# Transposes of a Perceiver-style kernel moved from TensorE to 32 by 32 blocks on VectorE, with copies and DMAs between the blocks

## The chip, the core and the metric

The kernel runs on one core of a Trainium2 chip. The metric is the device time of one execution in microseconds, taken as the median of several executions. A profile is one further execution recorded by the hardware profiler; its rows have times in us unless they are marked ns. The engines are PE (TensorE), DVE (VectorE), ACT (ScalarE), POOL (GpSimd) and SP (SyncE, which here only issues DMAs).

## The reference, cut to what matters

The input is x, 32 sequences of 64 tokens of width 256, and a context of 32 sequences of 256 tokens of width 256. Six residual blocks follow each other, all in float32:

```python
x = x + L0_xattn(ctx, layernorm(x))   # 16 heads of 64; keys and values from normalized context and x
x = x + L0_attn(layernorm(x))         # linear attention, 16 heads of 16
x = x + L0_ffn(layernorm(x))          # gated, hidden width 768
x = x + L1_xattn(layernorm(x), ctx, ctx, mask)   # 16 heads of 16, softmax over 256 context tokens
x = x + L1_attn(layernorm(x))         # sLSTM over the 64 tokens
x = x + L1_ffn(layernorm(x))          # 8 experts of width 1024, entmax gates
```

In both cross attentions, the softmax runs over the context tokens, so scores come out with the queries on the partitions and the context along the row. The product with the values sums over the context, so it needs the probabilities with the context on the partitions. That turn, and the turn of the context itself for the first attention's keys, are the transposes of this study.

## The kernel before

Tokens are held in 16 tiles of 128 (two sequences each), and all 16 stay in SBUF. The work falls into three stages.

**First cross attention** (`l0_context` to `l0_projected`, from line 774). It loops over the 16 tiles and in each over two batches. `l0_queries` handles a group of four batches at a time: it forms queries (banks `pq`) and folds the key weights into them (banks `pqk`, tiles `qk`). So scores are taken against the normalized context itself: `l0_keys` (line 855) turns the context of one batch with four PE transposes into a bank `tr_c` and copies it to the tile `cT`; a copy on POOL adds the 64 own tokens. `l0_scores` (line 869) forms eight banks `sc` of 128x320, takes a maximum on DVE and an exponential on ACT for each, scales on DVE, and turns the probabilities without PE: DVE transposes 32x32 blocks into `bT`, and 16 moves, one for each pair of block row and block column, carry the blocks into `pT`. Four of the moves are POOL copies, four go to ACT or DVE, and eight are DMAs. `l0_applied` (products `pu`) and `l0_projected` (`po`, `pw`) follow.

**Middle stage.** It loops over eight groups of two tiles: `linear_attention` (line 1092, names beginning with la), `feed_forward` (ff), `queries` (`xaq`), then for each tile `keys_values` (line 1245: loads the context already transposed, `ctxT`, into `xcT`, and forms `xak` and `xav`), and for each half of the heads `scores` (line 1274, banks `xsc`) and `weighted` (line 1313). `weighted` turns the probabilities with 16 PE transposes into four banks `xpTp`, copies each to SBUF, turns the reciprocal sums (`xrT`), and forms the products `xpo`. It then adds the value bias `vb` as it joins the two head halves. `projected` (`xpw`) and `slstm_router` (line 1365) follow.

**Experts.** The first twelve tiles' tokens go through gates and a first pass over eight experts, then the last four tiles' tokens and what was left over.

**What sets the order.** The kernel doesn't issue its instructions as it meets them. A planner (`Plan`, line 210) collects every operation with a rank, and `Plan.run` (line 299) lays them out one by one: of the operations whose inputs and places are there, it takes the one that can start first by its own table of durations (`PlanEngine.length`, line 474), and of equal ones that of lower rank. An operation whose rank is more than `ahead` (12.0, line 1863) above the lowest open rank has to wait. Operations given by `either` or `copy` may go to ACT or DVE. Each engine then runs its instructions in the order laid out, and SP issues its DMAs in that order too. Most instructions carry line 375, where the planner emits them, so the profile's groups are told apart by the names of their tiles and by their shapes. All SBUF tiles but a few are places in one large area, `arena`, given by `ar.put` (from line 646) with a tag, a size and one position for each buffer; a place is free again when all readers of its last tile are done.

## Time and profile before

| | |
|---|---|
| median of 3 runs | 1628.32 us (1628.05 to 1630.23) |
| the profiled execution | 1633.02 us |
| its span, first to last instruction | 1631.3 us |
| mean granted PE clock | 0.991 of full speed |
| PE, PEld (weight loads) | 1579.4 us, 1106.8 us busy |
| DVE, ACT, POOL | 1088.2, 693.8, 422.1 us busy |
| DMA | 95.02 MB, mean 58 GB/s |

A row of the slices shows the busy share of an engine in tenths for each of 40 equal parts of the span. A row of groups has the engine, the operation, output and input by name and shape, and a count; then its busy time in us and the mean duration of one in ns; then how long the engine stood idle in front of such an instruction, and what ended that. PE's instructions overlap each other, so the busy time of a group is less than its count times its mean. A product in float32 stands as two records for each instruction of the program; a transpose stands as one. A row of stretches has the length in us, the busy time and the number of instructions of each engine, the granted clock, the share of time that the DMA engines were busy, and GB/s.

### The profile page before, as it was taken

What the parts mean: (1) busy time and instruction counts of PE and PEld (TensorE: products, weight loads), DVE (VectorE), ACT (ScalarE), POOL (GpSimd) and SP (SyncE); (2) the same over time, 40 slices, a digit from 0 to 9 for tenths busy, and PEclk for the clock granted to TensorE, in tenths of its full rate; (3) what the DMA queues carried; (4) which work ended last, traced back from release to release, by engine and by line L of the source; (5) the groups of instructions that cost most, each with busy time, mean ns of one, the idle gap of its engine ahead of it and who ended that gap; (6) DMA issues with size and microseconds to landing.
All of it is one profiled execution on the core that took longest, in us unless ns stands there. A gap on an engine that the chain in (4) does not pass through costs nothing. (4 is left out here: it accounts for less than half of the span.)

```text
span 1631.3 us, 25951 instructions
## 1 busy us (share of the span) xinstructions
PE 1579.4 (97%) x9226; PEld 1106.8 (68%) x9226; DVE 1088.2 (67%) x3089; ACT 693.8 (43%) x1813; POOL 422.1 (26%) x524
## 2 busy tenths in 40 slices
PE   8999999999999999999989999999999999999996
PEld 6556656565665656666556777777777776878885
DVE  6657666676766757776755788888888788762230
ACT  4434344353533535334421454454544547432332
POOL 5123123230333223331311221221212112223342
PEclk9999999999999999999999999999999999999998
DMA  6112112121112211122121000010000220455391
GB/s 212 38 30 59 38 31 44 38 59 29 39 30 46 47 34 40 30 71 53 38 54 49 14 27 27 18 37 14 27 27 20 85 80 19 133 144 141 69 307 31
DMA packets 95601, 95.02 MB, mean 58 GB/s; under 512 B 9327, under 2 KB 85936, under 8 KB 95472
## 3 DMA queue, kind: packets, MB, share of 16 engines
q1 hardware_dynamic: 89952, 85.41, 19.2%
q0 software_dynamic: 5520, 7.94, 2.4%
q8 instruction: 74, 1.21, 0.3%
q14 instruction: 55, 0.45, 0.1%
HBM read 63.63 MB, written 7.47 MB: 44 GB/s over the span
## 5 line engine op out<-in xcount | busy, mean ns | idle before, releaser
L375 PE MATMUL pu<-arena 128*128 128x512 f32 (+1 forms) x768 | 301.0, 615 | 3.5 <-ACT arena L375 2.8
L375 PE MATMUL sc<-arena 128*128 128x320 f32 x1024 | 290.5, 436 | 0.0
L375 PEld LDWEIGHTS sc<-arena 128*128 128x128 f32 x1024 | 190.8, 190 | 95.3 <-issue 19.2
L375 ACT ACTIVATE arena<-sc,nmax 128x320 f32<-128x320 f32 x256 | 134.4, 527 | 250.3 <-DVE nmax L375 241.8
L375 PEld LDWEIGHTS pu<-arena 128*128 128x128 f32 (+1 forms) x768 | 113.9, 189 | 175.9 <-issue 159.1
L375 POOL COPY arena<-arena 32x640 f32<-32x640 f32 (+1 forms) x161 | 108.9, 676 | 404.1 <-DVE arena L375 300.4
L375 DVE TENSOR_REDUCE nmax<-sc 128x1 f32<-128x320 f32 x256 | 121.8, 484 | 105.5 <-PE sc L375 104.1
L375 POOL TENSOR_TENSOR arena<-arena 128x1024 f32<-128x1024 f32 (+3 forms) x72 | 118.5, 1646 | 166.6 <-DVE arena L375 109.7
L375 ACT ACTIVATE arena<-arena,xnm 128x256 f32<-128x256 f32 x256 | 127.1, 500 | 52.1 <-DVE xnm L375 51.9
L375 DVE COPY arena<-pu 128x512 f32<-128x512 f32 x62 | 42.7, 689 | 115.4 <-PE pu L375 115.2
L375 DVE CUSTOM_DVE_ANT_0 arena<-xsc,arena 128x256 f32<-128x256 f32 x256 | 101.2, 421 | 17.7 <-ACT arena L375 10.3
L375 DVE TENSOR_TENSOR arena<-arena,sm 128x1280 f32<-128x1280 f32 x64 | 108.1, 1690 | 2.2
L375 DVE STREAM_TRANSPOSE arena<-arena 128x512 f32<-128x512 f32 (+1 forms) x192 | 104.4, 594 | 3.6
L375 ACT COPY arena<-pu 128x512 f32<-128x512 f32 x66 | 38.4, 585 | 128.0 <-PE pu L375 128.0
L375 POOL DMA_INDIRECT out<-arena x25 | 39.6, 1585 | 102.8 <-DVE arena L375 71.2
L375 PE MATMUL pqk<-arena 64*128 64x256 f32 x512 | 63.1, 383 | 1.6 <-ACT arena L375 1.6
L375 PE MATMUL xpTp<-ident,arena 128*128 128x128 f32 x512 | 63.6, 274 | 0.9 <-ACT arena L375 0.9
L375 PE MATMUL xak<-arena 128*128 128x512 f32 x128 | 62.3, 610 | 0.0
L375 PEld LDWEIGHTS xpTp<-ident,arena 128*128 128x128 f32 x512 | 56.9, 141 | 7.2 <-DVE arena L375 2.2
L375 PE MATMUL xav<-arena 128*128 128x256 f32 x256 | 61.5, 384 | 0.0
L375 PEld LDWEIGHTS po<-arena 128*64 128x64 f32 x1024 | 55.5, 137 | 8.8 <-issue 8.3
L375 PE MATMUL mepha<-arena 128*128 128x256 f32 x256 | 60.1, 385 | 1.4 <-ACT arena L375 1.4
(395 smaller groups left out, 2800.9 us busy)
## 6 DMA issues: line engine op xcount, KB each, us to landing
arena<-in_m_w SPq DMA_DIRECT2D x26, 1024.0 KB
arena<-arena SPq DMA_DIRECT2D x256, 80.0 KB
arena<-in_ctx SPq DMA_DIRECT2D x32, 256.0 KB
arena<-in_ctxT SPq DMA_DIRECT2D x16, 512.0 KB
x<-in_x SPq DMA_DIRECT2D x16, 128.0 KB
arena<-in_l0x_wkv SPq DMA_DIRECT2D x2, 1024.0 KB
arena<-arena SPq DMA_DIRECT2D x16, 128.0 KB
out<-x SPq DMA_DIRECT2D x16, 128.0 KB
```

Of the source, the lines that this page charges most:

```text
L375: r = getattr(real, name)(*[get(a) for a in args], **{k: get(a) for k, a in kw.items()})
```

## The change

- **Context keys of the first attention.** For batches 1 to 31 `l0_keys` no longer uses PE. Two DVE transposes of 128x256 turn 32x32 blocks of the context into a new tile `bC`, and 16 moves of 32x128 carry them into `cT`: four by POOL, twelve by ACT or DVE. Batch 0 keeps the PE transposes. The columns of `cT`, and with them the blocks of the probabilities, stand in another order.
- **Probabilities of the second attention.** The 512 PE transposes and the 128 copies of `xpTp` go. For each half of a tile's heads, two DVE transposes of 128x1024 write `xbT`, and 16 moves of 32x512 fill `xpT`: four by POOL, four by ACT, eight by DMA. `xpr` has three places of 1024 instead of two of 2048, `xpT` one of 2048 instead of four of 512, `xbT` one, and `xcT` one instead of two.
- **Value bias.** It is folded into the output bias once, with two products (`pvb`), and the join of the two head halves becomes an addition on POOL.
- **sLSTM.** In seven of the eight groups, four small DVE operations move to POOL.
- **Planner.** A lean of 0.1 us against DVE where an operation may go to ACT or DVE; POOL copies have a shorter duration in its table; `ahead` is 10.0 instead of 12.0.
- **Places and order.** `wk` and `q` get other places (`q` is four quarter tiles), the linear attention's weights `a_wq` and `a_wkv` move to the places of `q` and are loaded late in the first stage, and the heads' groups are processed in plain order.

The diff, cut to its core:

```diff
-                    key = at, op.rank
+                    key = at + (self.lean if engine == "DVE" and len(op.ways) > 1 else 0.0), op.rank
...
-            return 0.7 if n < 64 else 0.3 + 2.0e-3 * n
+            return 0.7 if n < 64 else 0.15 + 0.97e-3 * n if name == "tensor_copy" else 0.3 + 2.0e-3 * n
...
-        ar.put(1, "q", 2048, 8192)
+        ar.put(0, "wk", 2048, 25856)
+        ar.put(1, "q", 512, 8192, 8704, 9216, 9728)
+        ar.put(1, "bC", 512, 42496, 43008)
...
-            ("xcT", 1024, 22016, 23040), ("xkT", 1024, 24064, 25088), ("xv", 1024, 30208, 31232),
-            ("xpr", 2048, 26112, 28160), ("xpT", 512, 35328, 35840, 36352, 36864), ("xne", 256, 37376, 37632, 37888),
+            ("xcT", 1024, 22016), ("xkT", 1024, 23040, 24064), ("xv", 1024, 30208, 31232),
+            ("xpr", 1024, 25088, 26112, 27136), ("xbT", 2048, 28160), ("xpT", 2048, 35328), ("xne", 256, 37376, 37632, 37888),
...
-            ("a_wq", 512, 42496), ("a_wkv", 1024, 43008), ("rows_a", 1024, 44032),
+            ("a_wq", 512, 8192), ("a_wkv", 1024, 8704), ("rows_a", 1024, 44032),
...
             if t == 2:
 
+                pl.rank = 29.5
...
+        def move(n, o, i, tight=False):
+
+            if n == 0:
+                pl.gpsimd.tensor_copy(o, i)
+            elif n == 1 and tight:
+                pl.scalar.copy(o, i)
+            elif n == 1:
+                pl.copy(o, i)
+            else:
+                pl.sync.dma_start(out=o, in_=i)
...
+            pl.rank = b - 2.6
+            cT = ar.tile([P, 5, KD, S], F32, tag="cT", name=f"cT{b}")
+            pl.gpsimd.tensor_copy(cT[:, 4], lt[:, :, b4 * S : (b4 + 1) * S])
...
+            bC = ar.tile([P, 4, KD, 2, B_], F32, tag="bC", name=f"bC{b}")
+            for i in range(2):
+                pl.vector.transpose(
+                    bC[:, :, :, i].rearrange("p k d c -> p d k c"),
+                    cx[:, 2 * b2 + i].rearrange("p (d k c) -> p d k c", d=KD, c=B_),
+                )
+            for n in range(4):
+                for a in range(4):
+                    k = (a + n) % 4
+                    move(
+                        min(n, 1),
+                        cT[B_ * k : B_ * k + B_, a].rearrange("p d c -> p (d c)"),
+                        bC[B_ * a : B_ * a + B_, k].rearrange("p d i c -> p (d i c)"),
+                    )
...
+        pl.vector.tensor_copy(vd, vb.unsqueeze(2).to_broadcast([P, 2, P]))
+        pl.lane = "vb"
+        pvb = bank([P, D], "pvb")
+        with pl.together(0.9):
+            for c in range(2):
+                mm(pvb, vd[:, c], x_wo[:, c, :], start=(c == 0), stop=(c == 1))
+        pl.vector.tensor_tensor(row("x_bo"), pvb, row("x_bo"), ALU.add)
...
+                pl.vector.transpose(
+                    bT[:, :, b2].rearrange("p k d j c -> p j d k c"),
+                    pr.rearrange("p j (d k c) -> p j d k c", d=2, c=B_),
+                )
+            pT = ar.tile([P, 4, 2, 2, 4, B_], F32, tag="xpT", name=f"xpT{nm}")
+            for n in range(4):
+                for a in range(4):
+                    k = (a + n) % 4
+                    move(
+                        n,
+                        pT[B_ * k : B_ * k + B_, a].rearrange("p b d j c -> p (b d j c)"),
+                        bT[B_ * a : B_ * a + B_, k].rearrange("p b d j c -> p (b d j c)"),
+                        tight=True,
                     )
...
-            for b2 in range(2):
-                for kc in range(2):
-                    pT = ar.tile([P, 4, P], F32, tag="xpT", name=f"xpT{nm}_{b2}_{kc}")
-                    pT_ps = bank([P, 4, P], f"xpTp{nm}_{b2}_{kc}")
-                    with pl.together(T4):
-                        for j in range(4):
-                            tr(pT_ps[:, j, :], pr[:, b2, j, kc * P : (kc + 1) * P], ident)
-                    pl.copy(pT, pT_ps)
-                    pTs[b2, kc] = pT
...
-            pl.vector.scalar_tensor_tensor(
-                oT[:, c], om[:, :, 0, :], vb[:, c : c + 1], om[:, :, 1, :], ALU.add, ALU.add
-            )
+            pl.gpsimd.tensor_tensor(oT[:, c], om[:, :, 0, :], om[:, :, 1, :], ALU.add)
...
+            side = pl.vector if g == NG - 1 else pl.gpsimd
+            side.tensor_scalar(il[:, :, :, 1:], il[:, :, :, 1:], 20.0, None, ALU.min)
...
-        pl.run(12.0)
+        pl.run(10.0)
```

## The prediction

> **What bounds the kernel now.** I read the page first: the busy shares, then the slices, because a mean over a kernel of three stages can hide a different limit in each.

> ```profile
> span 1631.3 us, 25951 instructions
> ...
> PE 1579.4 (97%) x9226; PEld 1106.8 (68%) x9226; DVE 1088.2 (67%) x3089; ACT 693.8 (43%) x1813; POOL 422.1 (26%) x524
> ...
> PE   8999999999999999999989999999999999999996
> ...
> DVE  6657666676766757776755788888888788762230
> ...
> PEclk9999999999999999999999999999999999999998
> ```

> TensorE (PE) is at nine tenths or more in 37 of 40 slices, at the full granted clock. VectorE (DVE) is next, and the only engine that comes near in the second half (slices 23 to 34). So I cut the span into stages and asked for each engine's busy time in each: first cross attention, change-over, the middle stage with the second cross attention, experts.

> ```profile
> core 0: us, PE busy (x) PEld busy (x) DVE busy (x) ACT busy (x) POOL busy (x), PEclk, DMA share, GB/s
> ...
> 80.00:840.00 760.00, 756.56 (x3632) 472.90 (x3631) 511.22 (x989) 315.83 (x767) 207.12 (x209) 1.00 0.19 43
> 840.00:880.00 40.00, 34.13 (x192) 22.53 (x189) 24.66 (x73) 8.36 (x16) 9.54 (x20) 0.91 0.25 66
> 880.00:1410.00 530.00, 520.42 (x4007) 389.40 (x4007) 427.99 (x1574) 269.56 (x783) 100.74 (x185) 1.00 0.11 36
> 1410.00:1631.30 221.30, 199.20 (x1106) 173.79 (x1104) 70.75 (x330) 63.13 (x159) 74.20 (x63) 0.96 0.50 140
> ```

> In the first attention PE idles 3.4 of 760 us, in the middle stage 9.6 of 530. Every microsecond taken off PE there is one off the time, as long as the others keep up. The page's chain of waits is of no use here: it ends at the last store on POOL and shows 0%. Third came the groups by shape, for durations.

> ```profile
> L375 POOL COPY arena<-arena 32x640 f32<-32x640 f32 x128 | 98.1, 766 | 304.3 <-DVE arena L375 300.4
> L375 DVE STREAM_TRANSPOSE arena<-arena 128x512 f32<-128x512 f32 x128 | 83.5, 690 | 3.6
> L375 PE MATMUL xpTp<-ident,arena 128*128 128x128 f32 x512 | 63.6, 274 | 0.9 <-ACT arena L375 0.9
> L375 ACT COPY arena<-arena 32x640 f32<-32x640 f32 x64 | 46.2, 722 | 18.6 <-DVE arena L375 17.2
> L375 DVE COPY arena<-xpTp 128x512 f32<-128x512 f32 x60 | 40.0, 685 | 4.5 <-PE xpTp L375 4.3
> L375 ACT COPY arena<-xpTp 128x512 f32<-128x512 f32 x68 | 38.6, 587 | 39.9 <-PE xpTp L375 39.8
> L375 DVE STREAM_TRANSPOSE arena<-arena 128x256 f32<-128x256 f32 x64 | 25.8, 402 | 0.0
> L375 PE MATMUL tr_c<-ident,arena 128*128 128x128 f32 x128 | 18.7, 276 | 0.0
> ```

> [...]PE's operations overlap, so its price is the busy time, 63.6/512 = 0.124 us a transpose, not the 274 ns that one lasts.

> **The PE work that goes.** All 512 xpTp transposes: 63.6 us. Of the 128 tr_c transposes 124 (batch 0 keeps its four): 18.7 x 124/128 = 18.1. The folded bias adds two 128x256 products, four PE records at 58.7/256 = 0.23 us (the pw group): 0.9. Net 80.8 us. If nothing came in their place the end would be 1628.3 - 80.8 = 1547.5. The profiled execution took 1633.0 around its span of 1631.3; the median is 1628.3, 0.3% below. I subtract from the median; the scale changes the sum by 0.3 us.

> **What comes instead, second attention.** Counts are from the built order of the changed program. DVE: 64 transposes of 128x1024, which no row shows; from 128x256 at 402 and 128x512 at 690 the slope is 1.125 ns an element, so 402 + 768 x 1.125 = 1.27 us each, 81. Gone from DVE: 60 copies, 40; 32 additions of 128x128 to GpSimd (POOL) at 0.340, 11; four s-LSTM steps in seven of eight groups at 0.386 + 3 x 0.334, 10. The lean of 0.1 us against DVE sends about 100 either-engine operations to ACT (31 relus at 0.386, 19 normalizations at 0.408, the rest 0.42 to 0.74): 46. DVE goes from 428 to 428 + 81 - 40 - 11 - 10 - 46 = 402. ACT: -39, +128 moves of 32x512, +about 47 for those operations. For the moves the row at 32x640 (722 ns) gives 578 in proportion and 722 at most; 0.61 x 128 = 78. ACT 270 to 356. POOL: 128 moves at about 0.65, 32 additions and the s-LSTM steps at about 0.5 to 0.7: +110, to 211. PE falls to 520.4 - 63.6 = 456.8. So DVE stands at 88% of PE's work instead of 82%, ACT at 78%, POOL at 46%: PE is still the longest, by less.

> [...]

> **The new wait.** Scores, transposes, moves and product of one half form a chain. Its prices come from a timeline of the first attention, where the same moves exist:

> ```profile
> 601.61 1.63 DVE L375 STREAM_TRANSPOSE arena<-arena 128x512 f32<-128x512 f32 x3
> ...
> 616.15 5.44 SPq L375 DMA_DIRECT2D arena<-arena  x8
> ...
> 616.18 3.19 POOL L375 COPY arena<-arena 32x640 f32<-32x640 f32 x4 [18.80 <-DVE arena L375]
> ...
> 625.39 3.17 PE L375 MATMUL pu<-arena 128*128 128x512 f32 x7
> ```

> Eight issues take 5.4 us; the packets in the trace end 1.2 us after the last. Eight exponentials at 0.50 + 0.19 keep ACT 5.5 us and start about 1 us into the 2.7 us of score products, so the last ends some 4 us after them; then 1.3 for the second transpose, 5.4 + 1.2 + 0.3 for the moves: about 12 us. In the built order PE has 13.7 to 29.5 us of other work between a half's scores and its product. Alone the chain is covered; with DVE at 88% its eight reductions and two transposes queue behind others, and the tightest halves (13.7 to 15.5) can stall.

> SP's queue also carries context loads, stores and expert weights: 256 new issues, 166 us of 457. A load that waits for PE holds the moves behind it.

> xcT, the transposed context, now has one place instead of two. The load of tile t+1 waits for the last value product of t, and on PE only 0.5 to 0.9 us of work stands between that and the first key product at five of the 15 changes; 2.3 at one, 3.4 or more at nine. A load moves 512 KB; in the trace its packets end 3.0 to 3.4 us after issue (154 GB/s in such a stretch), with the hop about 3.5. Stalls: 5 x 2.7 + 1.2 = 15 us. Bounds: 0, if PE is held elsewhere just then, and 30, if the load also queues behind a set of moves.

> For DVE's tightness I let the idle share of PE double from 9.6/530 to 3.6%: 457 x 0.036 - 9.6 = 7 us. Bounds 0 and 25.

> **What comes instead, first attention.** 62 transposes of 128x256 at 0.402: 25 us on DVE, less copies of tr_c and those leaned away (18 of 32x640 at 0.834, 9 of pu, 7 of tr_c: 26), plus 67 copies of 32x128 (at 0.17 in proportion to 32x640 to 0.3 with a fixed part, 11 to 20): about 525 in all. ACT gets 305 copies of 32x128, +18 of 32x640, +9 of pu, -24 of tr_c. No row has the small copy. [...] Keys start one batch earlier in rank; the context's affine step ends at 630.7 where its scores start at 646.0, and the 16 moves need about 5 us. I charge 2 us, bounds 0 and 10.

> **Ends.** The loads of a_wq and a_wkv (768 KB) leave the start for the last batches and stand in SP's order a batch (25 us) ahead of their products: nothing. The expert stage keeps its work; its third weight place now also waits for keys and probabilities, and the planner looks 10 ranks ahead instead of 12: 3 us, bounds -3 and 8. Sum: 80.8 - 15 - 7 - 2 - 3 = 54. 1628.3 - 54 = 1574.5, say **1575**.

> **Rivals.** *Nothing is given back*: 1547 to 1555; speaks for it the first attention's near perfect cover with DVE at 67%, against it the single xcT. Chance 0.18. *VectorE becomes the bound*: DVE's 402 us are 50 a group of two tiles, and each half's pair of transposes must wait for one xbT. POOL can lengthen DVE too: one 128x1280 product took 1.49 us alone and 2.94 beside a POOL product. If DVE operations grow by a fifth, 402 becomes 482 + 9.6, the middle stage shortens by 38 instead of 64, and with the other costs (15 + 2 + 3) the end is 1593; if the stage does not shorten at all, only 16 are left: 1612. I take 1603, between them; chance 0.17. *The chain becomes the bound, slower*: single xbT and xpT make halves serial. A group took 67.4 us for four halves, so it decides from 16.9 us a half. With 5.5 of scores, 2.5 transposes, 6.9 moves, 1.2 product and 2.5 of queueing, 18.6: 74.4 a group, +7 x 8 = 56, less 16: 1668. Against it stands that the scores of the next half need neither buffer. Chance 0.06. *No difference* 0.02.

> **How the numbers follow.** The main case, 1558 to 1592, has 0.57; with the first rival and most of the second the range 1550 to 1608 leaves about 2 in 10 out. Faster by over 0.2% (about what a measurement here tells from no change) are the first three, 0.92; within 0.02, slower 0.06.

> **What would show it.** Right: no xpTp group, four tr_c; PE about 1499 us busy, its idle in the middle stage about 30 us, with waits of the xak products on a DMA of in_ctxT; POOL's and ACT's copies up, idle. Wrong: PE busy under 90% there with the xpo products waiting on DVE or moves (the chain), or DVE at nine tenths with PE waiting for it (VectorE), or idle in front of sc (first attention).

## The result and the profile after

The changed kernel takes 1697.95 us (median of 4, 1689.05 to 1701.73), the kernel before 1628.18 beside it: a ratio of 1.042, 95% interval 1.0395 to 1.0443. The forecast was 1575 with a range to 1608. The profiled execution took 1694.88 us, its span 1693.2.

The page of the changed kernel, the lines that were read before (busy time and share, then tenths in 40 slices):

```profile
span 1693.2 us, 25872 instructions
...
PE 1556.5 (92%) x8594; PEld 1063.1 (63%) x8594; DVE 1089.9 (64%) x3047; ACT 866.5 (51%) x2265; POOL 553.4 (33%) x836
...
PE   7899999999999999999888998989989877889996
...
DVE  7566667666676666666565688868768677634131
...
PEclk9999999999999999999999999999989886899998
```

No engine has taken PE's place: DVE kept its busy time (1090 us, 1088 before), ACT is busy for half of the span and POOL for a third. PE has holes from slice 20 on, and its clock, at nine tenths or more in every slice but the last before, falls below that in slices 30 and 32 to 35, down to six tenths. Both show again in the windows of the stages (columns as before: busy us of each engine, then the granted clock):

```profile
80.00:840.00 760.00, 735.51 (x3459) 455.28 (x3458) 512.48 (x1065) 396.16 (x1046) 225.32 (x318) 0.99 0.19 44
840.00:880.00 40.00, 34.37 (x127) 19.37 (x126) 24.21 (x65) 12.08 (x28) 8.51 (x14) 0.96 0.21 47
880.00:1410.00 530.00, 473.17 (x3274) 335.88 (x3272) 388.83 (x1312) 311.21 (x819) 183.09 (x335) 0.94 0.22 61
1410.00:1693.00 283.00, 247.24 (x1457) 206.74 (x1457) 112.63 (x481) 104.89 (x269) 102.74 (x113) 0.90 0.46 131
```

In the middle stage PE idles 57 of 530 us instead of 10, and the granted clock is 0.94. DVE is busy for 73% of that stretch, 81% before, so the rival "VectorE becomes the bound" is out. The trace lists the stretches in which the clock was at half; with PE's records that splits a span into three sums: PE's busy time as it would be at full clock, the time lost at half clock (half of PE's busy time there: products of 128x256 for xav start 0.427 us apart in those stretches of the changed kernel, 0.216 at full clock, by the medians), and PE's idle time.

| us | PE work at full clock | lost at half clock | PE idle | span |
|---|---|---|---|---|
| before | 1571.4 | 7.9 | 51.9 | 1631.3 |
| after | 1502.7 | 53.8 | 136.7 | 1693.2 |
| difference | -68.7 | +45.9 | +84.8 | +61.9 |

So the PE work did go. More than it saved came back as idle time, and half as much again as a slower clock. The landmarks of the work say where (each cell: length, of it idle + lost at half clock):

| stretch | before | after |
|---|---|---|
| start to the pu products of batch 7 | 236.2: 11.9 + 1.5 | 243.9: 21.6 + 4.6 |
| to those of batch 31 | 617.8: 7.9 + 1.7 | 629.5: 22.3 + 7.0 |
| to the first xpw product of the middle stage | 87.0: 0.8 + 0.0 | 100.4: 7.2 + 1.4 |
| to the first slp product | 49.1: 0.8 + 0.0 | 53.8: 3.0 + 0.0 |
| four groups of four batches | 269.6: 4.0 + 0.0 | 271.6: 25.6 + 13.7 |
| three more, beside the experts' first half | 168.4: 5.0 + 0.0 | 212.0: 37.7 + 25.4 |
| to the end | 203.1: 21.6 + 4.8 | 182.0: 19.3 + 1.7 |

The first attention lost 19 us, the stretch between the attentions 13, the way from there to the first slp product 5, the four steady groups gained nothing from 33 us of PE work less, and the last two rows, which share their work out differently, lost 22 together. What PE waited for in the two stages (engine, tile, what ended the wait: us, times, longest), first of the first attention, then of the middle stage:

```profile
PE pqk L375 <- ACT arena L375: 14.1, 14, 1.4
PE laq L375 <- ACT arena L375: 4.6, 1, 4.6
```

```profile
PE xak L375 <- DMA arena<-in_ctxT: 7.1, 3, 3.0
PE xrT L375 <- POOL arena L375: 6.0, 2, 5.8
PE xsc L375 <- DVE x L375: 5.0, 1, 5.0
PE xak L375 <- DVE ve_lay L375: 5.0, 2, 2.5
PE xsc L375 <- ACT arena L375: 4.0, 5, 1.3
PE xav L375 <- DVE xnm L375: 3.9, 1, 3.9
...
PE xak L375 <- DVE arena L375: 2.9, 1, 2.9
```

These are many waits of many kinds. The three rows of xak give 15.0 us together. In front of the value products xpo, which end the chain of scores, moves and product, PE waits only 2.9 us in all. The name behind the arrow is not always the last cause: in a timeline of the changed kernel one gap has two names, VectorE's at the weight load and the DMA's at the product.

```profile
1098.72 1.67 PE L375 MATMUL xav<-arena 128*128 128x256 f32 x7
...
1100.42 0.33 SPq L375 DMA_DIRECT2D arena<-in_ctxT  x1
...
1103.81 0.30 PEld L375 LDWEIGHTS xak<-arena 128*128 128x128 f32 x2 [2.96 <-DVE ve_lay L375]
1103.85 1.68 PE L375 MATMUL xak<-arena 128*128 128x512 f32 x2 [2.59 <-DMA arena<-in_ctxT]
```

The load is issued as the last product on the one place of xcT ends (1100.4), and the product that needs it starts 3.4 us later. The 128x1024 transpose was forecast well: it lasts 1.24 us (1.27). The 32x128 copy, of which no row of before told, lasts 296 ns on ACT, 255 on DVE and 287 on POOL.

### The profile page after: what moved, and what is told of

Same layout as the page of the kernel before. It is cut to its first block, busy times and chain, and to the rows that moved or that the text cites. A ratio compares the mean times of both kernels' runs of the same rounds, so it can differ in the third digit from the quotient of the medians.

```text
span 1693.2 us, 25872 instructions
## 1 busy us (share of the span) xinstructions
PE 1556.5 (92%) x8594; PEld 1063.1 (63%) x8594; DVE 1089.9 (64%) x3047; ACT 866.5 (51%) x2265; POOL 553.4 (33%) x836
## 4 chain that ended last, share of the span: by engine, by line
PE 27%; DVE 12%; ACT 5%; DMA 3%; POOL 2%; issue 2%; SPq 0%; DVEq 0%; POOLq 0%; ACTq 0%
DVE arena L375 7%; ACT arena L375 5%; PE mepya L375 3%; PE mepha L375 3%; PE ffg L375 2%; PE xak L375 2%; PE xav L375 2%; POOL arena L375 2%; PE pu L375 2%; PE ffu L375 2%; PE lakv L375 1%; PE sc L375 1%; PE mepyb L375 1%; DVE x L375 1%; PE mephb L375 1%
## 5 line engine op out<-in xcount | busy, mean ns | idle before, releaser
L375 POOL COPY arena<-arena 32x640 f32<-32x640 f32 (+3 forms) x413 | 220.9, 537 | 563.1 <-PE sc L375 257.6
L375 PE MATMUL pu<-arena 128*128 128x512 f32 (+1 forms) x768 | 300.8, 615 | 4.5 <-DMA arena<-arena 3.2
L375 PE MATMUL sc<-arena 128*128 128x320 f32 x1024 | 291.3, 437 | 1.5 <-DVE arena L375 1.2
L375 ACT COPY arena<-arena 32x128 f32<-32x128 f32 (+2 forms) x515 | 228.2, 443 | 61.6 <-DVE arena L375 50.1
L375 PEld LDWEIGHTS sc<-arena 128*128 128x128 f32 x1024 | 191.5, 190 | 96.7 <-issue 17.6
L375 ACT ACTIVATE arena<-sc,nmax 128x320 f32<-128x320 f32 x256 | 133.7, 526 | 184.2 <-DVE nmax L375 183.2
L375 PEld LDWEIGHTS pu<-arena 128*128 128x128 f32 (+1 forms) x768 | 114.1, 189 | 176.2 <-issue 156.1
L375 DVE STREAM_TRANSPOSE arena<-arena 128x512 f32<-128x512 f32 (+2 forms) x318 | 208.3, 691 | 16.8 <-POOL arena L375 10.6
L375 POOL TENSOR_TENSOR arena<-arena 128x128 f32<-128x128 f32 (+3 forms) x125 | 135.7, 1089 | 187.1 <-DVE arena L375 144.4
L375 DVE TENSOR_REDUCE nmax<-sc 128x1 f32<-128x320 f32 x256 | 120.5, 482 | 98.6 <-PE sc L375 95.6
L375 ACT ACTIVATE arena<-arena,xnm 128x256 f32<-128x256 f32 x256 | 127.3, 500 | 49.1 <-DVE xnm L375 48.9
L375 DVE CUSTOM_DVE_ANT_0 arena<-xsc,arena 128x256 f32<-128x256 f32 x256 | 101.7, 417 | 26.5 <-ACT arena L375 22.1
L375 ACT COPY arena<-pu 128x512 f32<-128x512 f32 x75 | 42.7, 586 | 113.6 <-PE pu L375 113.6
L375 DVE TENSOR_TENSOR arena<-arena,sm 128x1280 f32<-128x1280 f32 x64 | 96.6, 1509 | 2.2
L375 PE MATMUL pqk<-arena 64*128 64x256 f32 x512 | 70.3, 409 | 14.1 <-ACT arena L375 14.1
L375 PE MATMUL xak<-arena 128*128 128x512 f32 x128 | 69.2, 674 | 14.9 <-DMA arena<-in_ctxT 7.1
L375 DVE COPY arena<-pu 128x512 f32<-128x512 f32 x53 | 36.0, 681 | 67.5 <-PE pu L375 67.5
L375 PE MATMUL xav<-arena 128*128 128x256 f32 x256 | 72.2, 433 | 5.9 <-DVE xnm L375 3.9
L375 PEld LDWEIGHTS pqk<-arena 64*128 64x128 f32 x512 | 53.2, 199 | 31.2 <-ACT arena L375 21.5
L375 PE MATMUL mepha<-arena 128*128 128x256 f32 x256 | 65.7, 411 | 5.2 <-DVE xnm L375 2.7
L375 POOL DMA_INDIRECT out<-arena x25 | 39.7, 1589 | 92.6 <-ACT arena L375 61.5
L375 ACT ACTIVATE arena<-arena 128x256 f32<-128x256 f32 (+3 forms) x59 | 23.2, 397 | 89.8 <-DVE arena L375 86.6
```

The lines of the kernel that those rows point to most:

```text
L375: r = getattr(real, name)(*[get(a) for a in args], **{k: get(a) for k, a in kw.items()})
```

## Experiments

The theory after the traces (A): gaps on PE, most of them in the middle stage, cost their own length and the clock behind them. Rivals: B, the keys' part with its small copies; C, the planner's three new constants (the lean against DVE, the length of a GpSimd copy, `ahead` 10); D, the chain of moves; later E, the moves as blocks in ScalarE's queue, and A', that beside the experts the transposes had covered VectorE's chains. Medians are in us; the ratio is to the kernel before, timed beside each. That kernel's own median moved between 1628.15 and 1633.59 from one session to the next, so where two runs come from different sessions, a difference of their medians can be off by some 5 us. The planner rearranges other work after most edits, so a single edit is rarely alone; where it was, the text says so.

### The two halves and the planner

**second_only**: keys of all batches by TensorE.

```
-            if b == 0:
+            if True:
```

> Only the second attention's part (and the sLSTM's moves and the planner's new constants) is left of the change; the context keys of all 32 batches go through TensorE again, 124 transposes or 18 us of PE work more than in the changed kernel. Theory A (the loss sits in the middle stage: PE gaps in front of xak, xsc, xrT, xav, about 61 us more idle there than before, and half-clock windows that such gaps set off): the first attention is back to 104.2 us per four batches, the 19 us lost by its end return, the middle stage keeps its groups of 70 us: 1679 to 1690 us, 1.03 to 1.04 of the kernel before. Theory B (the keys part, with its small ScalarE copies, is what costs): 1640 or less. Theory C (the planner's constants cost): about 1695, nothing gained.

1676.18, ratio 1.028 (1.0255 to 1.0309). That is 3 us below A's range and far from B and C: the first attention is back to 858 us (873 in the changed kernel, 854 before), and the middle stage is as in the changed kernel. The keys' half costs 22 us in the change.

**keys_only**: `scores`, `weighted`, the bias and the places of the second attention as before the change.

```
-        ("xcT", 1024, 22016), ("xkT", 1024, 23040, 24064)
+        ("xcT", 1024, 22016, 23040), ("xkT", 1024, 24064, 25088)
...
```

> Only the keys part (and the planner's new constants) is left of the change; the second attention's probabilities go through TensorE again. Theory A: the middle stage is as before (groups of 67.4 us, clock 0.99), the first attention and its end keep what they lost, 19 us: 1628 to 1648 us, 1.00 to 1.012 of the kernel before. Theory B (keys part): 1690. Theory C (planner's constants): above 1670 too. If neither half alone shows a loss, they cost only together, by the clock.

1673.72, ratio 1.026 (1.0237 to 1.0290). Theory A missed by 26 us, and C's mark for this run (above 1670) came true: the first attention lost 28 us, and the middle stage, with the code of before, still lost 20 us up to the eighth group (xpTp products waiting 11 us). One gap of the first attention in this kernel's trace, with rows left out:

```profile
339.57 2.14 ACT L375 COPY arena<-arena 32x128 f32<-32x128 f32 x7
...
341.74 1.56 ACT L375 COPY arena<-pqk 128x512 f32<-128x512 f32 x3
...
342.38 1.67 PE L375 MATMUL pqk<-arena 64*128 64x256 f32 x10 [0.61 <-ACT arena L375]
```

Seven of the keys' small copies stand in front of the ScalarE copies that free the pqk banks.

**keys_old**: keys_only with the planner's constants of before.

```
-        0.0, None, None, {}, 0.1
+        0.0, None, None, {}, 0.0
...
-    pl.run(10.0)
+    pl.run(12.0)
```

> Only the keys part, with the planner's three constants of before as well. If the planner's constants made the keys part lose (theory C for this half): the gaps in front of pqk shrink to some 6 us, the ones of 1.8 us in front of the second attention's transposes go, the half-clock windows with them: 1620 to 1640, 0.995 to 1.007 of the kernel before. If the keys part loses by itself (its 16 small copies a batch crowd ScalarE's copies out of the pqk banks): 1660 or more.

1635.29, ratio 1.004 (1.0025 to 1.0055). Theory C holds for this half: the constants alone cost 38 us, 18 of them in the first attention, and the four steady groups take the 269.6 us of before. The waits of the first attention, in the trace of this kernel:

```profile
PE pqk L375 <- ACT arena L375: 6.4, 7, 1.0
PE laq L375 <- ACT arena L375: 3.2, 1, 3.2
```

Still the keys' half gains nothing from 18 us of PE work less: the work at full clock is down by 8 only, idle up by 12.

**old_planner**: the whole change with those constants.

> The whole change, but with the planner's three constants of before (no lean towards ScalarE, the old length of a GpSimd copy, the old end offset). Theory A: the same places and the same chain, so the same gaps: 1685 to 1700. Theory C (the planner's constants made the order bad): below 1650, with the gaps of pqk and xsc gone.

1686.52, ratio 1.035 (1.0329 to 1.0379). In the range of A, far from C: in the whole change the constants are worth 11 us. The first attention regains 18 us, the stretches behind it give some 4 back in the profiles.

### One place for the transposed context

**xct2**: two places for xcT, the room from xTa.

```
-        ("xcT", 1024, 22016)
+        ("xcT", 1024, 22016, 16896)
-        ("xTa", 512, 42496, 43008)
+        ("xTa", 512, 43008)
...
```

> The whole change, but with two places for the transposed context (as before the change), so that the load for xak does not wait for the last xav of the batch pair before; the room is taken from xTa (one place). Theory A: the six xak gaps of 2.5 us (15 us in all) go, and with them the half-clock windows that begin right behind them (three to six of 3.4 us, 1.7 us lost in each): 1665 to 1677 us. If gaps elsewhere take their place (the moves' chain, theory D): 1685 or more. If more than 25 us come back, the gaps in front of xak set off most of the lost clock.

1675.74, ratio 1.029 (1.0259 to 1.0330): 22 us back, in A's range. PE's order is nearly the same (by tile names and shapes in the traces, 88 of 8594 records stand elsewhere). Idle time fell by 14.1 us and the loss at half clock by 11.4.

**second_xct2**: second_only with two places.

> The second attention's part with two places for the transposed context, and the context keys on TensorE for all batches. If the two losses add up (22 us less for the keys' half, 22 us less for the single place): 1650 to 1660. If what is left lies in the middle stage's other small gaps (about 35 us of idle time and 40 us of clock), it still stays above the kernel before.

1658.80, ratio 1.017 (1.0137 to 1.0211), 17 us below second_only. The two losses nearly add up (39 us of 44), and 29 us stay.

**before_xct1**: the kernel before with one place. In its trace the order on PE, DVE, ACT and POOL is instruction for instruction that of the kernel before, so here the edit is alone.

```
-        ("xcT", 1024, 22016, 23040)
+        ("xcT", 1024, 22016)
```

> The kernel before, whole, with one thing of the change alone: one place for the transposed context instead of two. Theory A (a single place makes TensorE wait for the load, about 2.5 us at each odd batch pair, and half-clock windows follow): 1640 to 1655, 1.007 to 1.016 of the kernel before. If the transposes that this kernel still has cover the load: 1626 to 1632.

1674.83, ratio 1.029 (1.0269 to 1.0303), more than expected: 47 us for one buffer by the medians, 39 between the two profiled executions. Its page and its waits:

```profile
PE 1589.6 (95%) x9226; PEld 1108.1 (66%) x9226; DVE 1087.9 (65%) x3089; ACT 695.8 (42%) x1813; POOL 422.5 (25%) x524
```

```profile
PE xak L375 <- DMA arena<-in_ctxT: 25.3, 7, 4.8
...
PE xak L375 <- DVE xsm L375: 3.6, 1, 3.6
```

The products are the same as before: of the 39 us, 29 are idle time, and PE is 10 us longer at its products. The clock changes on a grid of 3.41 us (shown at the end). Five windows of that grid that lie end to end over one of those gaps show why (length, PE busy, ..., granted clock, the third number from the right):

```profile
1022.19:1025.60 3.41, 3.41 (x32) 2.40 (x31) 2.44 (x11) 0.87 (x3) 0.71 (x1) 1.00 0.00 0
1025.60:1029.01 3.41, 1.04 (x5) 0.57 (x3) 3.11 (x14) 3.18 (x14) 0.33 (x1) 1.00 0.36 110
1029.01:1032.43 3.42, 2.17 (x3) 1.17 (x4) 1.68 (x8) 0.00 (x0) 1.86 (x3) 0.50 0.11 43
1032.43:1035.84 3.41, 3.41 (x18) 1.22 (x17) 0.00 (x0) 0.69 (x1) 0.00 (x0) 0.50 0.00 0
1035.84:1039.25 3.41, 3.41 (x55) 2.93 (x52) 1.98 (x7) 1.54 (x3) 0.00 (x0) 1.00 0.02 5
```

PE is busy for 1.04 of 3.41 us, the next window runs at half clock, and that one, only 2.17 busy, is followed by another. A gap of 3.6 us is followed by two windows at half clock.

**before_xct1_fill**: twelve products on data at hand in front of the product of each odd pair.

```
+                    for _ in range(12 if c == 0 and t % 2 else 0):
+                        mm(pk[:, 0:D], x_wk[:, 0, 0:P], x_wk[:, 0, :], start=True, stop=True)
```

> The kernel before with one place for the transposed context (1674.8 us), and at each odd batch pair twelve products of 128x256 on data at hand, into the bank that the late product then overwrites: 96 products of 0.223 us, 21.4 us of PE work added, all in front of the product that waits 3.6 us for the load, nothing else moved. If gaps set off the half clock (windows in which PE is busy less than half of the 3.41 us): the eight gaps shrink below 1 us, their half-clock windows go, and the time falls by 5 to 12 us, to 1663 to 1670, although work is added. If the clock has another cause: 1673 to 1677. If the added work is paid: 1690 or more.

1708.68, ratio 1.046 (1.0441 to 1.0481). Inconclusive by a mistake of mine: the gaps stand at the even pairs, right behind the last value product of the odd ones. The gaps stayed (27.3 us in front of xak), and twelve products are 24 records of 0.217 us, so 8 x 5.2 = 42 us were added and most of it was paid (34 us by the medians, 28 by the ratios). It says nothing about the clock.

### Are the missing transposes missed?

**xct2_fill**: xct2 with four groups of four transposes of constants in each half, wherever the planner puts them.

```
+            pl.lane = "f"
+            for n in range(4):
+                pf = bank([P, 4, P], f"fill{nm}_{n}")
+                with pl.together(T4):
+                    for j in range(4):
+                        tr(pf[:, j, :], x_wo[:, 0, 0:P], ident)
```

> The changed kernel with two places for the transposed context, and 512 transposes of constant data that nobody reads put into the second attention, as many as the change removed (63 us of PE work at full clock), which the planner may put wherever TensorE is free. Theory A (the transposes removed were the cover of other waits, and their absence costs idle time and clock): the time stays within 1640 to 1690 although 63 us of work are added, the clock goes back to 0.98 or more. Rival (PE work is what bounds it, clock and gaps have another cause): 1720 or more.

1712.93, ratio 1.050 (1.0466 to 1.0538), between the two theories: 57 us of work more at full clock, 37 us of time. A third of the work vanished in gaps, two thirds were paid. A's forecast of a clock of 0.98 or more missed too: it was 0.966. In the four steady groups PE's idle time fell from 21.2 to 11.9 us. In the stretch beside the experts' first half it stayed (31.8 and 31.2 us), although PE had 30 us more work there. Filling wherever the planner puts it is no cure.

### The moves

**xct2_nodma**: xct2 with all moves by copies (`move(n % 2, ...)` for `move(n, ...)`).

> The changed kernel with two places for the transposed context, the eight moves of each half of the second attention that go by DMA given to GpSimd and ScalarE instead (256 copies of about 0.62 us each more). Theory D (the DMAs' issue of 5 us and landing of 2 us in the chain from the scores to the products cost): 1655 to 1668. Theory A without D: the chain's length is not what is missing: 1672 to 1690, ScalarE's 80 us more work makes its other waits longer.

1733.43, ratio 1.064 (1.0604 to 1.0666), 58 us above xct2, outside both ranges. Without any DMA in the chain it got worse, against theory D. But the 256 copies more, at 616 ns on ScalarE and 618 on GpSimd in this kernel's trace, are some 160 us of work, so this run does not price the DMAs alone.

**s2x_noact**: second_xct2 with ScalarE's moves given to DMAs as well (`n and max(n, 2)` for `n`: twelve DMAs, four GpSimd copies). The reason for it, in the trace of second_xct2, ACT and then PE:

```profile
1368.75 2.53 ACT L375 COPY arena<-arena 32x512 f32<-32x512 f32 x4
1371.31 0.56 ACT L375 ACTIVATE arena<-xaq,arena,hm 128x256 f32<-128x256 f32 x1
```

```profile
1371.93 1.70 PE L375 MATMUL xsc<-arena 32*128 32x256 f32 x8 [2.91 <-ACT arena L375]
```

The last of the copies that make the queries stands behind four moves, and PE behind that copy.

> The second attention's part with two places for the transposed context and the keys on TensorE (1658.8 us), with the four moves of each half that ScalarE copies given to DMAs, so twelve DMAs and four GpSimd copies. Theory E (the moves stand as blocks of 2.5 us in ScalarE's queue, in front of copies that TensorE waits for; 128 of them, 79 us, in the middle stage): 1635 to 1652, with PE's waits for ScalarE in the middle stage less than half. Theory D (four more DMA issues, 2.5 us, make the chain from scores to products longer, and that chain is what is late): 1662 to 1685.

1643.76, ratio 1.009 (1.0075 to 1.0111): 15 us back, as theory E had it. The four steady groups now take 253.9 us against 269.6 before. But PE's waits that end on ACT fell less than expected (from 22.6 to 16.0 us between 850 and 1500), and in the traces 898 of 8718 records stand elsewhere in PE's order, so part of the gain may be the order's. Twelve DMAs instead of eight did not make it slower, against theory D.

**s2x_old**: second_xct2 with the planner's constants of before.

> The same second attention's part with the planner's three constants of before. If the constants cost in this half as they did in the keys half (38 us there): 1630 to 1645. If their cost there was one of the first attention's (its pqk copies) alone: 1650 to 1665, the middle stage with the same gaps in other places.

1653.74, ratio 1.015 (1.0128 to 1.0163). The constants cost 5 us in this half by the medians, and the intervals of the two runs overlap; in the other half they cost 38.

**s2x_side**: second_xct2 with the sLSTM's small operations on VectorE (`side = pl.vector`).

> The same second attention's part with the sLSTM's small operations back on VectorE. If GpSimd's queue (the moves and the sLSTM's operations, in front of the additions and masks that the products wait for) is what is late: 1640 to 1652. If not: 1655 to 1668, VectorE having some 1 us more in each group of four batches.

1666.72, ratio 1.024 (1.0221 to 1.0255), 8 us above second_xct2. GpSimd's share of them does no harm.

**noact_ra**: s2x_noact with the product of reciprocals and mask written ahead of the moves.

> The second attention's part with two context places, the keys on TensorE and ScalarE free of moves (1643.8 us), with the product of the sums' reciprocals and the head mask put ahead of the moves in the program, so that GpSimd does it first. If xrT's wait for GpSimd (9.1 us in 7 gaps, the largest one left after xpo) is real lateness: 1630 to 1638. If another wait ends right behind it: 1640 to 1647.

1666.74, ratio 1.022 (1.0185 to 1.0250): both expectations missed. The wait for GpSimd did go, from 9.1 to 1.3 us between 850 and 1500, and the time rose by 23 (20 by the ratios). The four steady groups (254 us of each), s2x_noact and then this kernel:

```profile
1011.00:1265.00 254.00, 232.85 (x1792) 168.93 (x1793) 217.19 (x725) 135.57 (x400) 108.13 (x197) 1.00 0.31 80
```

```profile
1011.00:1265.00 254.00, 233.44 (x1691) 165.93 (x1691) 208.66 (x700) 128.09 (x375) 103.27 (x187) 0.96 0.30 79
```

PE is idle equally long in both, 21 us. In one the gaps never set off the half clock; in the other they do, and the stretch up to the fourth group took 264.4 us instead of 253.9. The same idle time, placed differently, went with 10 us more.

### Where the experts lie beside the attention

**hyb_tail**: s2x_noact with TensorE's transposes for the last six batch pairs.

```
+                if t < 10:
                     pl.vector.transpose(
...
+            if not (t < 10):
+                for b2 in range(2):
+                    for kc in range(2):
+                        pT_ps = bank([P, 4, P], f"xpTp{nm}_{b2}_{kc}")
...
```

> The same 1643.8 us version, with TensorE's transposes again for the last six of the 16 batch pairs (192 transposes, 24 us of PE work more at full clock), where the experts' first half lies beside them. Theory A' (in that stretch the transposes covered the entmax and routing chains of VectorE, and without them 28 us of idle time and 24 us of clock are lost): the time falls to 1612 to 1632 although 24 us of work are added. If the stretch's loss comes from other parts of the change (the order, GpSimd's share): 1655 to 1670.

1625.32, ratio 0.9964 (0.9943 to 0.9986): 21 us of work at full clock put back, the time 18 us down, in the range of theory A'. The stretch beside the experts is idle for 6.8 us and loses 3.4, instead of 32.5 and 24.2. That stretch in s2x_noact, then in this kernel:

```profile
1265.00:1467.90 202.90, 170.43 (x1141) 126.67 (x1141) 130.46 (x471) 89.17 (x261) 74.34 (x125) 0.86 0.42 115
1261.60:1415.80 154.20, 147.35 (x1228) 112.28 (x1227) 111.46 (x449) 93.84 (x273) 40.11 (x72) 0.98 0.22 69
```

The edit puts PE work in, but it also takes the moves and VectorE's transposes out: DVE (third of the busy times) is 19 us less busy there, POOL (last) 34, and the DMA engines' share falls from 0.42 to 0.22. So it shows that the new path costs in this stretch. It does not show that the transposes' time had covered anything: with the moves kept, more PE work did not mend it (xct2_fill).

**hyb_mid**: blocks and moves for pairs 2 to 9 only, the value bias on VectorE.

> Block transposes and moves only for batch pairs 2 to 9, where the middle stage is steady; TensorE's transposes in pairs 0, 1 and 10 to 15, and the value bias added on VectorE as before the change. Theory A': the 15.7 us that the steady part gains (253.9 against 269.6 us) are left and the stretches around it are as before: 1608 to 1622, faster than both kernels. If the stretches lose all the same: 1640 or more.

1640.28, ratio 1.006 (1.0036 to 1.0082). The stretch between the attentions is mended (89.6 us), but the four groups, laid out in another order, take 275.8 with the half clock back (11 us). The forecast of 1608 to 1622 missed.

**hyb_mid_ra**: the same with noact_ra's edit.

> As hyb_mid, with the product of the reciprocals ahead of the moves on GpSimd: 2 to 6 us below hyb_mid if GpSimd's order matters in the steady part, within 2 us of it otherwise.

1646.28, ratio 1.009 (1.0052 to 1.0119): 6 us above hyb_mid, so both expectations missed; the two intervals overlap.

**hyb_tail_late**: hyb_tail with the bias's product at a later rank.

```
+        rank_, pl.rank = pl.rank, R0 - 1.0
         pl.vector.tensor_copy(vd, vb.unsqueeze(2).to_broadcast([P, 2, P]))
...
+        pl.rank = rank_
```

> The fastest version (1625.3 us: block transposes and moves for batch pairs 0 to 9, TensorE's transposes for the last six, keys on TensorE, two context places, no moves on ScalarE), with the value bias's product planned some 20 products later, behind the first keys of the context, where its weights have landed. If its wait for the weights (3.0 us) and the half-clock windows behind it are what the stretch loses: 1616 to 1623. If the other waits of that stretch end as late: 1623 to 1628.

1620.99, ratio 0.9924 (0.9910 to 0.9937), below both kernels and in the first expectation. The stretch between the attentions takes 95.4 instead of 103.3 us, and nothing there is lost at half clock. Its page:

```profile
PE 1538.9 (95%) x8910; PEld 1068.1 (66%) x8910; DVE 1058.8 (66%) x2944; ACT 724.8 (45%) x1892; POOL 488.7 (30%) x664
...
PE   8999999999999999999999989999899999999995
...
PEclk9999999999999999999999999999999999999998
```

The mean granted clock is nearly back to that of before (0.989, 0.991), with 44 us less PE work; PE's idle time is 77 us, 52 before, and the time is 13 us shorter.

## Why the prediction was wrong

The step that failed is "every microsecond taken off PE there is one off the time, as long as the others keep up". Their mean shares kept up. Their results came late all the same: the forecast gave back 27 us for stalls of every kind, and PE's idle time rose by 84.8. The half clock, for which it had no term, took another 45.9, so each us of idle time was paid about one and a half times. Term by term:

- **PE work, 80.8.** It came to 68.7. Most of the 12 us between them is the price: a group's busy time counts moments that it shares with its neighbours. If each moment of PE is counted for one product only, the transposes that went hold 73 us of the kernel before, not 81.7. This term was nearly right.
- **The clock, no term.** It took 45.9 us, against 61.9 between the two spans. The kernel before lost 7.9, and its clock row gave no cause to look; the prediction's own 27 us of stalls should have.
- **The single place, 15 us.** The stall was right: six gaps, 15.0 us of idle time in front of xak. Its price was not: 22 us (xct2), 47 in the kernel before (before_xct1).
- **The middle stage, 7 us for a tight VectorE.** The size was far too small, and a nearly full VectorE was not the reason. From the first xpw product to the eighth group's slp, its work fell by 3 us only (395 to 392) where 26 were forecast for the middle stage, and stood at 91% of PE's work at full clock (88% taken). But the stretch grew, and VectorE was busy for 73% of it, 81% before. Of PE's 53 us of waits there, without those of xak, 28 end on VectorE, 15 on ScalarE and 8 on GpSimd. Two places are known. Copies behind ScalarE's moves cost 15 us with the order that came with it (s2x_noact). Beside the experts, 57 us were idle or lost in s2x_noact, and 10 with the old path back (hyb_tail).
- **The first attention, 2 us, at most 10.** The keys' half cost 22 us (second_only). No run shows the 2 us, which were an estimate of mine. The prediction counted ScalarE's copies (in the changed kernel that engine is busy for 396 of 760 us, 316 before) and not its queue: small copies stand in front of the copies that free the pqk banks (the rows under keys_only). Up to the last batch's pu products, PE's waits that end on ScalarE are 5 us before, 26 after and 4 in second_only. How bad that is hangs on the planner's constants (18 us of it between keys_only and keys_old), which the prediction priced at no more than its 3 us for the ends. Which of the three does it was not tried.
- **Ends, 3 us.** The stretch between the attentions lost 13. The bias's product waits there for its weights (3.2 us on a DMA), and planned later it gave some 8 back in that stretch (hyb_tail against hyb_tail_late); the prediction counted its 0.9 us of work and not its place in the queue.
- **The slower rival, 1668 with 0.06,** had the sign and one of its marks, PE busy for under 90% (473 of 530 us), and not the mechanism: PE waits only 2.9 us in front of xpo in the changed kernel. With twelve DMAs in the chain it waited some 10 us there (s2x_noact), and the kernel still got faster.
- **The VectorE rival's 1612** leaves out the 5 us charged for the first attention and the ends, which its 1593 subtracts; this changes nothing in the outcome.

What stays open: why the new path costs so much for the six pairs beside the experts and not for the ten others. In s2x_noact 19 of the 32 us of waits there end on VectorE, which also runs the routing. Whether the transposes' time had covered these waits, or the moves and VectorE's new transposes delay the work that PE waits for, was not separated.

## What to carry to other kernels

When an engine is busy for 97%, work taken off it is worth its length only if what it waits for still comes in time (here 68.7 us went and 84.8 us of idle time came), and mean busy shares do not show that; before counting on it, look in the built order for what stands directly behind each piece that goes, and in the other engines' queues for what stands in front of the copies it waits for. Count a forecast stall of TensorE with the clock that follows it (45.9 us lost at half clock came with those 84.8). And give up the second buffer of a load last: in the kernel before, one place changed the busy times of DVE, ACT and POOL by 2 us at most and PE's by 10, and cost 47 us.
